# A graph layer on one core: one fixed order for the gather stage, readers further behind the gathers, and other buffers around it

## The chip, the cores and the metric

The kernel runs on one core of a Trainium2 chip. The metric is the device time of one execution in microseconds (us), smaller being better; the median of several runs is compared. A core has five engines with a program each: PE (TensorE, matrix products), DVE (VectorE), ACT (ScalarE), POOL (GpSimd) and SP (SyncE, here only an issuer of transfers). They run side by side and wait for one another by semaphores. Transfers (DMA) are issued from the queues of SP, ACT and POOL.

## The reference

A graph layer over 12500 nodes with 256 features and 200000 edges, sorted by their target node:

```python
h = relu(layernorm(x))                                   # 12500 x 256
agg = segment_sum(h[src], dst, num_segments=12500)       # 200000 gathered rows
z = (1 + eps) * h + agg
t = relu(batchnorm(z @ W1 + b1, g1, bt1))                # 12500 x 512
y = relu(batchnorm(t @ W2 + b2 + h, g2, bt2))            # 12500 x 256
return x + y
```

A batchnorm takes its mean and variance over all nodes, so each of the two ends a stage: nothing behind it can start before the last node's row is known.

## The kernel before

**Tiles.** The 200000 edges are 1563 tiles of 128, taken in 131 groups of GT = 12. As the edges are sorted by target, a group's targets lie close together: group i is taken to lie in a window of WIDE = 128 + 2 x 76 = 280 nodes that begins at 96 i - 76 (`span`, STEP = 96). A short stage at the start checks this on the device and sets a flag; a second program for other data (`general`) isn't run here. The 12500 nodes are 25 chunks of 512.

**Start.** dst and src are loaded as whole numbers (L146 to L158): each as a block of whole rows in one or two transfers, a short last row in one more, and the places behind it filled with zeros first. dst goes through SP's queue and DVE's fill, src through ACT's queue and POOL's fill; ACT's queue also carries the small vectors and the two weight matrices. They are turned so that each column holds one tile's indices; the checks and the flag follow.

**The gather stage** (most of the time). Its parts, by name:

- `gather(i)` (L391 to L401): twelve indirect transfers on POOL, L398, each fetching 128 rows by src into one buffer `gt`; there are AHEAD + 1 = 5 such buffers. For the first LEAD = 24 groups the rows come from x, and `settle` (L338 to L357) normalises them in place (six bn_stats on DVE, a root on ACT, reciprocal and product on DVE, twelve activations on ACT); later groups read the table h_tab.
- `h_chunk(g)` (L370 to L388): makes a chunk of h from x by the same `settle`, stores it in h_tab, transposes it on PE (L381), copies it out of PSUM (L385, L387) and stores it in h_cols.
- `sums(i)` (L419 to L436): DVE builds a 0/1 matrix `oh` from the targets (L423), PE adds up the group's rows per target in `ps` with twelve matmuls (L433), which the profile shows as 24 records.
- `join(i)`: ACT copies `ps` to `zs` (L440), DVE builds the placing matrix `at` (L442). `put(i)`: PE places the sums in the window, `pz` (L452). `add(i)`: DVE adds `pz` into the chunks `zc` that the window touches (L465). `z_chunk` loads such a chunk from h_cols and scales it by 1 + eps (L412).
- `first_layer(c)`: once no later window touches chunk c, PE multiplies it with W1 in four slices (L474), DVE takes bn_stats (L478), ACT copies the slice to `ts` (L479), and one transfer of 1 MB stores the chunk in t_tab (L480).

The loop L488 to L509 writes these down in the order h_chunk, gather(i+4), join(i-1), put(i-1), settle(i), sums(i), add(i-1), first_layer. The compiler's scheduler then sets each engine's order; on PE it places the first two tiles of the next group's sums ahead of put, and the rest behind it. Buffers: gt 5, oh 2, zs 3, at 2, ps 2, pz 1, ts 2.

**Second layer.** `ti` reads t_tab back and `yT` reads h_cols (SP's queue, L531, L532), ACT normalises (`tT`, L535), PE multiplies with W2 (L542), DVE adds h and takes statistics. Before its end, XAHEAD = 10 chunks of x are loaded. **Output.** ACT normalises (L560), PE transposes, DVE adds x, ACT's queue stores; each step loads one more chunk of x.

Of the kernel before, what the change touches and what calls it, by code (L numbers as in the profile page):

```python
# [7 lines left out]
F32 = mybir.dt.float32  # L8
I32 = mybir.dt.int32
AF = mybir.ActivationFunctionType  # L10
OP = mybir.AluOpType
PSUM = bass.MemoryType.PSUM
# [3 lines left out]
R = 4  # L16
EPS = 1e-5
GT = 12
MARGIN = 76
AHEAD = 4  # L20
LEAD = 24
XAHEAD = 10

# [7 lines left out]
def kernel(  # L31
# [103 lines left out]
    with ExitStack() as es:  # L135
# [7 lines left out]
        safe = whole // 32 * 32  # L143
        assert PU <= P and whole < PU and PU - safe <= 32
        raws = {}
        for name, arr, eng in (("d", dst, nc.sync), ("s", src, nc.scalar)):  # L146
            raws[name] = ti = raw.tile([P, PART], I32, name="rawi_" + name)
            (nc.vector if name == "d" else nc.gpsimd).memset(ti[safe:PU, :], 0)
            if safe:
                eng.dma_start(ti[:safe, :], arr[: safe * PART].rearrange("(p e) -> p e", e=PART))  # L150
            if whole > safe:
                eng.dma_start(
                    ti[safe:whole, :], arr[safe * PART : whole * PART].rearrange("(p e) -> p e", e=PART)
                )
            if rest:
                eng.dma_start(
                    ti[whole : whole + 1, :rest], arr[whole * PART :].rearrange("(o e) -> o e", o=1)
                )  # L158
# [121 lines left out]
    def fast():  # L280
# [24 lines left out]
        with ExitStack() as fs:  # L305
# [8 lines left out]
            with ExitStack() as es:  # L314
# [4 lines left out]
                tsp = es.enter_context(tc.tile_pool(name="ts", bufs=2))  # L319
                ps_h = es.enter_context(tc.tile_pool(name="ps_h", bufs=1, space=PSUM))  # L320
                ps_i = es.enter_context(tc.tile_pool(name="ps_i", bufs=1, space=PSUM))
                ps_s = es.enter_context(tc.tile_pool(name="ps_s", bufs=2, space=PSUM))
                ps_z = es.enter_context(tc.tile_pool(name="ps_z", bufs=1, space=PSUM))
                ps_t = es.enter_context(tc.tile_pool(name="ps_t2", bufs=2, space=PSUM))

                col_i = keep.tile([P, WIDE], I32, name="col_i")
# [32 lines left out]
                xts = {}  # L359
# [10 lines left out]
                def h_chunk(g):  # L370
                    n = chunks[g][1] * R
                    slots = len(parts[g])
                    x_chunk(g + 2)
                    ht = ln.tile([P, R, D], F32, name="ht")
                    settle(xts.pop(g), -(-slots // 2), slots, ht, "c")
                    carry(nc.scalar, ht, h_tab, g, store=True)
                    hc = ln.tile([P, DC, CH], F32, name="hc")
                    for d in range(DC):
                        ph = ps_h.tile([P, CH], F32, name="pc")
                        for c in range(slots):  # L380
                            nc.tensor.transpose(  # L381
                                ph[:, c * P : (c + 1) * P], ht[:, c, d * P : (d + 1) * P], ident
                            )
                        if d % 2:
                            nc.scalar.copy(hc[:, d, :n], ph[:, :n])  # L385
                        else:
                            nc.vector.tensor_copy(hc[:, d, :n], ph[:, :n])  # L387
                    nc.sync.dma_start(h_cols[g, :, :, :n], hc[:, :, :n])  # L388
# [15 lines left out]
                zc = {}  # L404

                def z_chunk(c):
                    if c in zc or c >= NCH:
                        return
                    n = chunks[c][1] * R
                    zc[c] = zcp.tile([P, DC, CH], F32, name="zc")  # L410
                    nc.sync.dma_start(zc[c][:, :, :n], h_cols[c, :, :, :n])
                    nc.scalar.activation(zc[c][:, :, :n], zc[c][:, :, :n], AF.Copy, scale=gin1)  # L412

                def span(i):
                    return STEP * i - MARGIN, STEP * i - MARGIN + WIDE

                summed, placed = {}, {}

                def sums(i):  # L419

                    t0, n = groups[i]
                    oh = sel.tile([P, GT, P], F32, name="oh")
                    nc.vector.tensor_tensor(  # L423
                        oh[:, :n, :],
                        col[:, :P].unsqueeze(1).to_broadcast([P, n, P]),
                        dstT[:, t0 : t0 + n].unsqueeze(2).to_broadcast([P, n, P]),
                        op=OP.is_equal,
                    )
                    ga = gathered.pop(i)
                    ps = ps_s.tile([P, D], F32, name="ps")  # L430
                    for j in range(n):
                        rows = left if t0 + j == full_tiles else P
                        nc.tensor.matmul(  # L433
                            ps, lhsT=oh[:rows, j, :], rhs=ga[:rows, j, :], start=(j == 0), stop=(j == n - 1)
                        )
                    summed[i] = ps  # L436

                def join(i):
                    zs = sel.tile([P, D], F32, name="zs", bufs=3)
                    nc.scalar.copy(zs, summed.pop(i))  # L440
                    at = sel.tile([P, WIDE], F32, name="at")
                    nc.vector.tensor_scalar(  # L442
                        at, col, shift[:, i : i + 1], None, op0=OP.is_equal
                    )
                    placed[i] = zs, at

                def put(i):

                    zs, at = placed.pop(i)
                    pz = ps_z.tile([P, DC, CH], F32, name="pz2")  # L450
                    for d in range(DC):
                        nc.tensor.matmul(  # L452
                            pz[:, d, :WIDE], lhsT=zs[:, d * P : (d + 1) * P], rhs=at, start=True, stop=True
                        )
                    return pz

                def add(i, pz):
                    lo, hi = span(i)
                    for c in range(max(lo, 0) // CH, -(-min(hi, N) // CH)):
                        z_chunk(c)  # L460
                        a, b = max(lo, c * CH, 0), min(hi, (c + 1) * CH, N)
                        if a >= b:
                            continue
                        side = zc[c][:, :, a - c * CH : b - c * CH]
                        nc.vector.tensor_add(side, pz[:, :, a - lo : b - lo], side)  # L465
                    z_chunk(max(lo, 0) // CH + 1)

                def first_layer(c):
                    n = chunks[c][1] * R
                    ts = tsp.tile([P, HC, CH], F32, name="ts")  # L470
                    for f in range(HC):
                        ph = ps_t.tile([P, CH], F32, name="ph")
                        for d in range(DC):
                            nc.tensor.matmul(  # L474
                                ph[:, :n], lhsT=w1s[:, d, f * P : (f + 1) * P],
                                rhs=zc[c][:, d, :n], start=(d == 0), stop=(d == DC - 1),
                            )
                        nc.vector.bn_stats(st1[:, f, c, :], ph[:, :n])  # L478
                        nc.scalar.copy(ts[:, f, :n], ph[:, :n])  # L479
                    nc.scalar.dma_start(t_tab[c, :, :, :n], ts[:, :, :n])  # L480
                    del zc[c]

                x_chunk(0)
                x_chunk(1)
                for i in range(min(AHEAD, NG)):
                    gather(i)
                made = done = 0
                for i in range(NG + 1):  # L488

                    while made < NCH and made < 2 + NCH * i // (LEAD - AHEAD):  # L490
                        h_chunk(made)
                        made += 1
                    if i + AHEAD < NG:
                        gather(i + AHEAD)
                    pz = None
                    if i > 0:
                        join(i - 1)
                        pz = put(i - 1)
                    if i < NG:
                        if i < LEAD:  # L500
                            settle(gathered[i], GT // 2, GT, gathered[i], "g")
                        sums(i)
                    if i == 0:
                        continue
                    add(i - 1, pz)
                    nxt = span(i)[0] if i < NG else N
                    while done < NCH and min((done + 1) * CH, N) <= nxt:
                        first_layer(done)
                        done += 1  # L509
# [4 lines left out]
            late = fs.enter_context(tc.tile_pool(name="late", bufs=1))  # L514
            yT = [late.tile([P, DC, w * R], F32, name=f"yT{g}") for g, (_, w) in enumerate(chunks)]

            xin = fs.enter_context(tc.tile_pool(name="xin", bufs=XAHEAD))
            xrs = []

            def x_rows(g):  # L520
                if g < NCH:
                    xrs.append(xin.tile([P, R, D], F32, name="xr"))
                    carry(nc.sync, xrs[g], x, g, store=False)

            with tc.tile_pool(name="tin", bufs=3) as tin, tc.tile_pool(name="tsb", bufs=2) as tsb, tc.tile_pool(
                name="ps_y", bufs=4, space=PSUM
            ) as ps_y:
# [26 lines left out]
            with tc.tile_pool(name="ysb", bufs=3) as ysb, tc.tile_pool(name="ps_o", bufs=3, space=PSUM) as ps_o:  # L554
                for g in range(NCH):
# [18 lines left out]
                    x_rows(g + XAHEAD)  # L574
# [251 lines left out]
```

## Time and profile before

| what | value |
|---|---|
| three runs | 2607.53, 2616.31, 2614.66 us |
| median | 2614.66 us |
| the profiled execution: time, and span in the trace | 2590.8 us, 2589.0 us |
| start, until the first gather | 26.35 us |
| gather stage: first gather to the end of the last | 26.35 to 2294.5 us |
| from there to the first matmul of the second layer | 2342.66 us |
| second layer, until the first output activation | 2515.29 us |
| output | to 2589.0 us |

A group of instructions is shown on the page as line, engine, operation, tiles written and read, number, busy time, mean ns of one, then the idle time of its engine just before them and what ended most of it. The row of slices gives a busy share in tenths for each fortieth of the span, 64.7 us. A row of the timeline gives start, length, engine, line and operation, and in brackets the idle time before it and what ended that. The granted TensorE clock over the whole run is 0.767 of full speed.

The waits that the trace adds up over the whole span (waiting engine and line, what ended the wait, us in total, times, longest):

```profile
ACT zs L440 <- remote: 1256.0, 76, 38.9
DVE oh L423 <- remote: 904.9, 75, 22.6
PEld pz L452 <- ACT zs L440: 686.3, 65, 38.2
```

"remote" is a releaser that the trace doesn't name. And two stretches, of the gather stage and of the second layer (start and end, length, then busy time and number of PE, PEld, DVE, ACT and POOL instructions, the granted clock, the DMA engines' share, GB/s):

```profile
1200.00:1400.00 200.00, 112.93 (x395) 84.08 (x393) 41.98 (x54) 11.46 (x22) 135.21 (x143) 0.77 0.36 110
2350.00:2400.00 50.00, 50.00 (x118) 22.20 (x117) 19.80 (x29) 20.83 (x29) 0.00 (x0) 1.00 0.88 330
```

### The profile page before, as it was taken

To read this page: it belongs to the slowest core of one execution; us is meant where nothing else is said; L and a number is where in the kernel's file an instruction comes from. 1 tells how busy PE (TensorE), PEld (TensorE's weight loads), DVE (VectorE), ACT (ScalarE), POOL (GpSimd) and SP (SyncE) were. 2 spreads that over 40 slices of the span, in tenths; PEclk is the share of its full clock that TensorE was granted. 3 is DMA by queue.
4 is the path that set the end of the run, shared out by engine and by line. 5 is a ranking of instruction groups with operands and counts; after the bars stand their busy time and mean duration, and the time that the engine had idled before them with its cause. 6 is when DMAs were issued, how large, how long until landed. Compare 5 with 4: busy or idle time off the path is not lost.

```text
span 2589.0 us, 14795 instructions
## 1 busy us (share of the span) xinstructions
PE 1435.9 (55%) x4873; PEld 1021.2 (39%) x4873; DVE 711.9 (27%) x1059; ACT 467.4 (18%) x885; POOL 1482.4 (57%) x1576
## 2 busy tenths in 40 slices
PE   1255575554654545464745544555564555478985
PEld 1243353432433334343534433443343434353444
DVE  5244464421221212121212211221121221133444
ACT  3254465500000000000000000000000000014434
POOL 4655466666666666666666666666666666720000
PEclk9667687776877777677877777777776777788996
DMA  6455575433333333333333333333333333328728
GB/s 193 141 179 166 175 232 161 132 113 95 118 120 113 93 121 115 91 118 119 114 95 120 113 119 94 115 114 92 121 116 92 117 112 110 96 78 335 265 85 301
DMA packets 147183, 349.41 MB, mean 135 GB/s; under 512 B 28917, under 2 KB 81241, under 8 KB 140953
## 3 DMA queue, kind: packets, MB, share of 16 engines
q0 software_dynamic: 75008, 204.90, 26.7%
q1 hardware_dynamic: 41146, 90.41, 10.2%
q10 hardware_dynamic: 30942, 53.06, 5.5%
q8 instruction: 41, 0.67, 0.1%
q14 instruction: 46, 0.37, 0.0%
HBM read 284.26 MB, written 64.00 MB: 135 GB/s over the span
## 4 chain that ended last, share of the span: by engine, by line
another core or an unknown queue 51%; PE 26%; ACT 7%; issue 7%; DMA 4%; DVE 3%; POOL 1%; ACTq 0%; SPq 0%; POOLq 0%; DVEq 0%
PE ps L433 10%; PE py L542 6%; PE ph L474 5%; PE pz L452 4%; ACT gt L355 3%; DMA out_dram<-ot 1%; ACT zs L440 1%; POOL gt L398 1%; DMA zc<-h_cols 1%; ACT ht L355 1%; ACT zc L412 1%; DVE oh L423 1%; DVE st L478 1%; PE po L566 1%
## 5 line engine op out<-in xcount | busy, mean ns | idle before, releaser
L398 POOL DMA_INDIRECT gt<-h_tab,srcT x1275 | 1206.2, 946 | 608.5 <-issue 371.9
L433 PE MATMUL ps<-gt,oh 128*128 128x256 f32 x3126 | 789.9, 414 | 74.9 <-ACT gt L355 61.1
L433 PEld LDWEIGHTS ps<-gt,oh 128*128 128x128 f32 x3126 | 665.2, 213 | 198.3 <-ACT gt L355 65.1
L452 PE MATMUL pz<-at,zs 128*128 128x280 f32 x524 | 215.9, 549 | 770.1 <-ACT zs L440 660.3
L423 DVE TENSOR_TENSOR oh<-col,dstT 128x1536 f32<-128x1536 f32 x131 | 229.0, 1748 | 1143.3 <-remote 904.9
L452 PEld LDWEIGHTS pz<-at,zs 128*128 128x128 f32 x524 | 123.2, 252 | 834.9 <-ACT zs L440 686.3
L398 POOL DMA_INDIRECT gt<-in_x_dram,srcT x288 | 273.0, 948 | 180.8 <-ACT zs L440 96.1
L440 ACT COPY zs<-ps 128x256 f32<-128x256 f32 x131 | 48.8, 372 | 1613.7 <-remote 1256.0
L474 PE MATMUL ph<-zc,w1s 128*128 128x512 f32 (+1 forms) x400 | 214.6, 689 | 188.7 <-issue 145.3
L474 PEld LDWEIGHTS ph<-zc,w1s 128*128 128x128 f32 x400 | 86.4, 225 | 298.4 <-issue 241.5
L465 DVE TENSOR_TENSOR zc<-pz,zc 128x560 f32<-128x560 f32 (+9 forms) x203 | 100.8, 526 | 340.6 <-remote 167.8
L542 PE MATMUL py<-tT,w2s 128*128 128x512 f32 (+1 forms) x400 | 169.6, 587 | 12.0 <-ACT tT L535 12.0
L355 ACT ACTIVATE gt<-gt,nbg,rsg 128x256 f32<-128x256 f32 x288 | 149.5, 590 | 4.1 <-DVE nbg L353 1.8
L542 PEld LDWEIGHTS py<-tT,w2s 128*128 128x128 f32 x400 | 76.4, 192 | 105.2 <-issue 86.9
L478 DVE BATCH_NORM_STATS2 st<-ph 128x6 f32<-128x512 f32 (+1 forms) x100 | 67.2, 681 | 154.3 <-PE ph L474 64.5
L344 DVE BATCH_NORM_STATS2 stg<-gt 128x6 f32<-128x512 f32 x144 | 91.5, 688 | 33.4 <-DMA gt<-in_x_dram,srcT 23.2
L479 ACT COPY ts<-ph 128x512 f32<-128x512 f32 (+1 forms) x100 | 57.4, 575 | 197.1 <-DVE st L478 147.3
L535 ACT ACTIVATE tT<-ti,of,sc 128x512 f32<-128x512 f32 (+1 forms) x100 | 72.1, 792 | 99.8 <-issue 90.7
L381 PE MATMUL pc<-ident,ht 128*128 128x128 f32 x196 | 39.3, 334 | 53.6 <-issue 22.0
L442 DVE TENSOR_SCALAR at<-col,shift 128x280 f32<-128x280 f32 x131 | 65.4, 499 | 0.3 <-PE pz L452 0.3
L546 DVE TENSOR_TENSOR yT<-py,yT 128x512 f32<-128x512 f32 (+1 forms) x50 | 33.9, 677 | 109.2 <-PE py L542 107.2
L381 PEld LDWEIGHTS pc<-ident,ht 128*128 128x128 f32 x196 | 28.5, 171 | 72.1 <-issue 28.5
(80 smaller groups left out, 396.9 us busy)
## 6 DMA issues: line engine op xcount, KB each, us to landing
t_tab<-ts ACTq DMA_DIRECT2D x24, 1024.0 KB
ti<-t_tab SPq DMA_DIRECT2D x24, 1024.0 KB
gt<-h_tab,srcT POOLq DMA_INDIRECT x1275
xt<-in_x_dram SPq DMA_DIRECT2D x24, 512.0 KB
h_tab<-ht ACTq DMA_DIRECT2D x24, 512.0 KB
h_cols<-hc SPq DMA_DIRECT2D x24, 512.0 KB
zc<-h_cols SPq DMA_DIRECT2D x24, 512.0 KB
yT<-h_cols SPq DMA_DIRECT2D x24, 512.0 KB
```

Of the source, the lines that this page charges most:

```text
L344: nc.vector.bn_stats(st[:, c : c + 2, :].rearrange("p c s -> p (c s)"), v[:, c : c + 2, :].rearrange("p c d -> p d c"),)
L355: nc.scalar.activation(to[:, c, :], v[:, c, :], AF.Relu, bias=nb[:, c : c + 1], scale=rs[:, c : c + 1])
L398: nc.gpsimd.indirect_dma_start(out=ga[:rows, t - t0, :], out_offset=None, in_=x if i < LEAD else h_tab, in_offset=bass.IndirectOffsetOnAxi ...
L423: nc.vector.tensor_tensor(oh[:, :n, :], col[:, :P].unsqueeze(1).to_broadcast([P, n, P]), dstT[:, t0 : t0 + n].unsqueeze(2).to_broadcast([P ...
L433: nc.tensor.matmul(ps, lhsT=oh[:rows, j, :], rhs=ga[:rows, j, :], start=(j == 0), stop=(j == n - 1))
L440: nc.scalar.copy(zs, summed.pop(i))
L452: nc.tensor.matmul(pz[:, d, :WIDE], lhsT=zs[:, d * P : (d + 1) * P], rhs=at, start=True, stop=True)
L465: nc.vector.tensor_add(side, pz[:, :, a - lo : b - lo], side)
L474: nc.tensor.matmul(ph[:, :n], lhsT=w1s[:, d, f * P : (f + 1) * P], rhs=zc[c][:, d, :n], start=(d == 0), stop=(d == DC - 1),)
L478: nc.vector.bn_stats(st1[:, f, c, :], ph[:, :n])
L535: nc.scalar.activation(tT[:, f, :n], ti[:, f, :n], AF.Relu, bias=of1[:, f : f + 1], scale=sc1[:, f : f + 1],)
L542: nc.tensor.matmul(py[:, :n], lhsT=w2s[:, f, d * P : (d + 1) * P], rhs=tT[:, f, :n], start=(f == 0), stop=(f == HC - 1),)
```

## The change

- **Window.** MARGIN is 64 for 76, so WIDE is 256 for 280, which the data still fits.
- **Edge loads.** dst and src both go through SP's queue, each as one block, one short row, and one more transfer that fills the rest of that row with edges from the front of the array; no zero fill.
- **Order.** In the gather stage the scheduler no longer orders: each engine runs the instructions as they are written. A step i is: gather(i+4); add(i-4); `take` (bn_stats, copy and store) of the slice made in the step before; spots(i-2) and hold(i-2), the two halves of the old join; edges(i+1), which builds `oh`; h_chunk(i); settle(i+1); z_scale; sums(i); the transposes and copies of chunk i-1 (`turn`, `turn_out`); put(i-2); z_load; and at most one slice of the first layer.
- **Buffers.** oh 3, at 3, ht 3, ps 3, pz 2. `ts` holds one slice, four of them, each stored by its own transfer of 256 KB. The transposes share the slices' two PSUM buffers.
- **Lead-in.** LEAD is 30 for 24; one chunk of h per step for 25 steps instead of 25 in 20 steps.
- **Later stages.** The buffers of ti, tT and four more x chunks lie at the other end of the memory, apart from the gather stage's, and each tile waits for its own place to come free rather than for a whole pool. Four more chunks of x (XMORE) are loaded before the output stage.

```diff
-MARGIN = 76
+MARGIN = 64
-LEAD = 24
+LEAD = 30
+XMORE = 4
...
+        for name, arr in (("d", dst), ("s", src)):
+            raws[name] = ti = raw.tile([P, PART], I32, name="rawi_" + name)
+            nc.sync.dma_start(ti[:whole, :], arr[: whole * PART].rearrange("(p e) -> p e", e=PART))
+            for at, e0, n in ((0, whole * PART, rest), (rest, 0, PART - rest)):
+                if n:
+                    nc.sync.dma_start(
+                        ti[whole : whole + 1, at : at + n], arr[e0 : e0 + n].rearrange("(o e) -> o e", o=1)
+                    )
...
-                ps_h = es.enter_context(tc.tile_pool(name="ps_h", bufs=1, space=PSUM))
-                ps_s = es.enter_context(tc.tile_pool(name="ps_s", bufs=2, space=PSUM))
-                ps_z = es.enter_context(tc.tile_pool(name="ps_z", bufs=1, space=PSUM))
+                ps_s = es.enter_context(tc.tile_pool(name="ps_s", bufs=3, space=PSUM))
+                ps_z = es.enter_context(tc.tile_pool(name="ps_z", bufs=2, space=PSUM))
+                es.enter_context(tc.manual_schedule())
...
+                def take(c, f):
+                    n = chunks[c][1] * R
+                    ph = slices.pop((c, f))
+                    nc.vector.bn_stats(st1[:, f, c, :], ph[:, :n])
+                    ts = tsp.tile([P, CH], F32, name="ts")
+                    nc.scalar.copy(ts[:, :n], ph[:, :n])
+                    nc.scalar.dma_start(t_tab[c, :, f, :n], ts[:, :n])
...
+                for i in range(NG + 4):
+                    before = added
+                    if i + AHEAD < NG:
+                        gather(i + AHEAD)
+                    late = 4 if i < NG else 3
+                    while added <= min(i - late, NG - 1):
+                        add(added)
+                        added += 1
+                    for c, f in taken:
+                        take(c, f)
+                    taken = []
+                    if 0 <= i - 2 < NG:
+                        spots(i - 2)
+                        hold(i - 2)
+                    if i + 1 < NG:
+                        edges(i + 1)
+                    if i < NCH:
+                        h_chunk(i)
+                    if i + 1 < min(LEAD, NG):
+                        settle(gathered[i + 1], GT // 2, GT, gathered[i + 1], "g")
+                    for c in scales.get(i, ()):
+                        z_scale(c)
+                    if i < NG:
+                        sums(i)
+                    if 0 < i <= NCH:
+                        turn(i - 1)
+                        turn_out(i - 1)
+                    if 0 <= i - 2 < NG:
+                        put(i - 2)
+                    for c in loads.get(i, ()):
+                        z_load(c)
...
-            with tc.tile_pool(name="tin", bufs=3) as tin, tc.tile_pool(name="tsb", bufs=2) as tsb, tc.tile_pool(
+            with tc.tile_pool(name="tin", bufs=3, side="right", reuse_waits="tile") as tin, tc.tile_pool(
+                name="tsb", bufs=2, side="right", reuse_waits="tile"
...
+                for g in range(XAHEAD, XAHEAD + XMORE):
+                    x_rows(g)
...
-                    x_rows(g + XAHEAD)
+                    x_rows(g + XAHEAD + XMORE)
```

## The prediction

> **What bounds the kernel now.** I read the page's shares first, then the slices, the groups, the waits, and last the timeline of one stretch.
>
> ```profile
> span 2589.0 us, 14795 instructions
> PE 1435.9 (55%) x4873; PEld 1021.2 (39%) x4873; DVE 711.9 (27%) x1059; ACT 467.4 (18%) x885; POOL 1482.4 (57%) x1576
> POOL 4655466666666666666666666666666666720000
> DMA  6455575433333333333333333333333333328728
> ```
>
> No engine is full. GpSimd is at six tenths in every slice until it ends in slice 36, so nearly the whole span is one stage that POOL's gathers run through; the DMA engines are a third busy there, so bytes don't set it. The groups and waits say what POOL lacks:
>
> ```profile
> L398 POOL DMA_INDIRECT gt<-h_tab,srcT x1275 | 1206.2, 946 | 608.5 <-issue 371.9
> L398 POOL DMA_INDIRECT gt<-in_x_dram,srcT x288 | 273.0, 948 | 180.8 <-ACT zs L440 96.1
> L452 PE MATMUL pz<-at,zs 128*128 128x280 f32 x524 | 215.9, 549 | 770.1 <-ACT zs L440 660.3
> ...
> POOL gt L398 <- issue: 453.9, 1478, 2.1
> POOL gt L398 <- remote: 206.3, 53, 6.2
> POOL gt L398 <- ACT zs L440: 105.7, 17, 15.0
> ```
>
> A gather takes 0.95 us and an issue gap of 0.30; between waits the timeline has their starts 1.25 us apart, and twelve, one group, take 15.0 us. 1563 gathers at 1.2508 are 1955 us. The first starts at 26.35 and the last ends at 2294.5, which is 2268: POOL waits 313 us. In two windows: up to 480 us, 288 gathers in 454 us against 360 (94 lost); from 480 to 2294.5, 1275 in 1814.5 against 1595 (220 lost). So a group takes 17.1 us in the long part, not 15.0. The one bound that stays if every wait goes is 15.0.
>
> What POOL waits for is a free gt buffer, which the sums of five groups earlier release. The landed data is four groups ahead, so the chain sums, zs copy, at, pz, add is late:
>
> ```profile
> 1207.89 5.34 PE L433 MATMUL ps<-gt,oh 128*128 128x256 f32 x24
> ...
> 1227.61 0.95 POOL L398 DMA_INDIRECT gt<-h_tab,srcT  x1 [0.30 <-issue]
> 1231.87 0.37 ACT L440 COPY zs<-ps 128x256 f32<-128x256 f32 x1 [25.21 <-remote]
> 1231.87 1.76 DVE L423 TENSOR_TENSOR oh<-col,dstT 128x1536 f32<-128x1536 f32 x1 [21.96 <-remote]
> 1232.11 0.94 POOL L398 DMA_INDIRECT gt<-h_tab,srcT  x1 [3.55 <-remote]
> 1232.30 2.23 PE L452 MATMUL pz<-at,zs 128*128 128x280 f32 x4 [19.06 <-ACT zs L440]
> ```
>
> The matmuls are recorded as over at 1213.2, yet zs (ACT), the next oh (DVE) and POOL all go on only at 1231.9, with PE idle between. Other groups go on at once. I found no cause in the trace; the lateness of PE's completion is the unknown that decides this case. In the order of before it holds up everything, as pz of a group stands in front of the next group's sums and waits for its zs.
>
> **Part 1, the order of the stage.** A step now makes sums(i), then put(i-2), then at most one slice of the first layer; adds come four behind, gathers four ahead; oh, zs, at, ps, pz have two or three buffers. What is left of the wait is judged by each engine's load. PE: in the window 480 to 2280 it is busy 940.9 us for 106 groups, 8.9 a group, sums, pz and slices together. DVE 365.4 (3.4 a group) and ACT 121.5 (1.1). All stand under 15.0, so in the steady part POOL should be the bound; gather(i+4) needs sums(i-1), which leaves PE nearly three groups, 45 us, for a lateness of up to 24. Worth: the 220 us. 1275 x 1.2508 = 1595.
>
> A rule that speaks against this: PEclk reads 0.75 in that window. The Trainium skill ("TensorE: Matmul & The Clock Gate", Part 1) says that an idle window of about 3.4 us drops the clock to half and about 3.4 us of work brings it back. The new order spreads PE's work over each step with some 6 us free, so the gate could close in every step. By the row, a group costs 8.9. By the rule at its worst, half clock throughout, 8.9 x 0.75 / 0.5 = 13.4 us, an estimate, still below 15.0. I take the row: the clock moves PE but not the end.
>
> **Part 2, lead-in of 30 groups and one chunk of h per step.** Six more settled groups add 6 x (6 x 0.688) = 25 us to DVE and 6 x (12 x 0.59) = 42 to ACT; both lie beside POOL's 15.0 a group. The question is one step's ping-pong with both a chunk and a group. ACT: ts 0.58, zs 0.37, root 0.29, a DVE answer 0.34, four ht 2.36, a wait for six bn_stats (4.10 less 2.36), root 0.30, answer 0.36, twelve gt 7.09, zc scale 1.14, hc 0.58: 15.15, with hops 15.6. From the other side, with sums at half clock (24 x 0.43 = 10.3, the slow records of that group, whose mean is 0.414) the DVE copy of hc, which now waits behind them, delays the next step: 12.3 + 0.7 + 5.1 of DVE's work ahead of the next root, less 1.24, is 16.9. Over 25 steps: (15.6 - 15.0) x 25 = 15 to (16.9 - 15.0) x 25 = 47 us, of which gathers run ahead hide some 27. Loss 0 to 37; I take 10, where before loses 94. h_tab's last chunk is made in step 24 (about 25 x 15.6 + 40 = 430); gather(30) comes at 23.5 + 360 x 1.2508 = 474, so the table is there.
>
> **Part 3, slices, ts and t_tab.** 100 stores of 256 KB for 25 of 1 MB. The rule against it ("SBUF — State Buffer", The DMA setup-cost knee): each transfer pays about 2 us however small, so coalesce. By the rule: 75 more x 2 = 150 us if it were serial. By the rows: an issue on ACT's queue takes 0.33, 75 more are 25 us on an engine with 1.1 us of work per 15 us step, and a 1 MB load (ti) starts tT 5.0 us after issue, so a quarter of it lands well within a step with four ts buffers. Cost 0; without that cover, in the last eight slices, 0 to 5 us.
>
> **Part 4, the end of the stage.** From the last gather's end to the first second-layer matmul before: 2342.66 - 2294.5 = 48.2, of which five waiting groups take some 30 (6.1 us each) and the ti load ends last:
>
> ```profile
> 2336.75 11.14 SPq L531 DMA_DIRECT2D ti<-t_tab  x5
> 2341.79 5.75 ACT L535 ACTIVATE tT<-ti,of,sc 128x512 f32<-128x512 f32 x8 [9.09 <-DMA ti<-t_tab]
> ```
>
> ti, tT now lie apart from the stage's buffers, so the loads can come before the norm is done (2333.5): 8 us go. No backlog: landing 2, last sums 1.7, three hops of hold, put, add at 2.5, a chunk's four slices 7.0, the last chunk with norm 6.7, tT 0.9: 26. I take 30 (23 to 42).
>
> **Part 5, the start.** src's small loads are issued at 10.37 and 10.82, behind ten other loads on ACT's queue, its cast starts at 16.01, the flag falls at 24.27, of which DVE's rel (until 18.1) bounds part. On SP's queue behind dst they come by about 9, so the cast by 13. Two fills (1.48 POOL, 1.45 DVE) go, two small loads come. Gain 2.5 to 3, bounds -4 to +5; I take the first gather at 23.5.
>
> **Part 6, more x early.** Second layer: PE back to back, unchanged. In the last 74 us DMA's share is 0.81, so 2 MB of x that move ahead of it are worth 0 (hidden) to 2 MB / 277 GB/s = 7.6; I take 3. WIDE 256 for 280: pz and at shrink by 9%, off the path.
>
> **Sum.** 23.5 + 1955 + 10 = 1988.5; + 30 = 2018.5 for the second layer; before's rest, 2589.0 - 2342.66 = 246.3, less 3: 2262 of span. The profiled run was 2590.8, 1.8 over its span: 2264. The runs' median, 2614.66, is 0.9% above the profiled run; whether that lies in waits that go or in the pace I can't tell, so I add two thirds: **2280**.
>
> **Rivals.**
> - *PE's lateness is PE's own, and still ends part of the steps.* For: it strikes three waiters at once, and nothing in the order explains it. Against: from 2291, gathers over, five groups ran at 6.1 us without it. hold(i-2) waits behind the ts copy of the last slice, so a slice late by 19 makes a step of 19 + 5 = 24, one on time 10; if 45% are late, 16.3 on the mean. Over 101 groups: 2280 + 1.3 x 101 = **2410**. If all of the 17.1 stays, only lead-in, tail and start gain: 2280 + 2.1 x 101 = 2490.
> - *Slower: the fixed order chains the engines.* In each step ACT's hold, DVE's edges and the bn_stats stand behind the same slice, and next the sums behind edges; a late slice stops all three, where the scheduler's order had something between. Four of five steps late: 0.8 x 24 + 0.2 x 10 = 21.2, over 101 groups 2280 + 6.2 x 101 = **2906**. It decides against the change from a mean step of 15.0 + (2615 - 2280) / 101 = 18.3, that is, when about 60% of slices are late. Before, 63 of 106 zs in the long window waited on "remote", 18 us each, which is near that point; but most of those stand behind pz, and two groups' slack wasn't there.
> - *It does nothing:* the waits only change their names, the order being data-bound. Lead-in, tail and start alone would still give 2490, so within 0.3% (which is about what a measurement can tell from none) needs a loss that cancels them: **2610**.
>
> **Chances.** Forecast 0.55 (own range 2240 to 2340), PE's lateness 0.28 (2340 to 2490), slower 0.14, nothing 0.03. The range runs over the first two, to 2470. Faster 0.84, same 0.02, slower 0.14.
>
> **What would show it.** Right: POOL near eight tenths in its slices, gather idle by issue alone (0.30 a gather), the last gather by 2000, zs idle without effect on POOL, ti landed before the norm's end. Part 2 wrong: POOL waits before 480 us on gt. Rival one: POOL still waits on "remote" or PE after 500 us, 16 us a group. Slower: the waits name ts or oh, and POOL falls under six tenths.

## The result, and the profile after

The medians of five runs each are 2564.79 us after and 2610.16 before. The ratio is 0.9824, with a 95% interval of 0.9803 to 0.9844. The change gains 1.8%, 45 us, a seventh of the 335 us forecast. The profiled run spans 2563.9 us, against 2589.0 before. Three lines of its page and three of its waits (waiting engine and line, what ended the wait, us in total, times, longest):

```profile
POOL 4666666666666666666666666666666666610000
...
L406 POOL DMA_INDIRECT gt<-h_tab,srcT x1203 | 1138.6, 947 | 565.3 <-issue 364.0
...
L467 PE MATMUL pz<-at,zs 128*128 128x256 f32 x524 | 176.8, 461 | 430.2 <-ACT zs L456 330.5
```

```profile
DVE st L496 <- remote: 914.4, 45, 37.8
POOL gt L406 <- issue: 481.3, 1503, 5.7
POOL gt L406 <- remote: 195.8, 36, 6.6
```

POOL is still at six tenths and still loses 196 us to a releaser without a name. The wait has a new name on DVE: bn_stats of the slice, first in the new order to need PE, waits where zs did.

The same trace shows what such a wait is made of. From the timeline (start, length, engine, operation, idle time before it), with lines left out:

```profile
1199.73 2.54 PE L449 MATMUL ps<-gt,oh 128*128 128x256 f32 x11
...
1203.27 0.47 PE L449 MATMUL ps<-gt,oh 128*128 128x256 f32 x1 [0.34 <-issue]
...
1206.06 0.38 PE L449 MATMUL ps<-gt,oh 128*128 128x256 f32 x1 [1.73 <-issue]
...
1212.25 0.94 POOL L406 DMA_INDIRECT gt<-h_tab,srcT  x1 [0.30 <-issue]
1213.06 0.58 PE L449 MATMUL ps<-gt,oh 128*128 128x256 f32 x1 [2.21 <-issue]
1215.15 0.58 PE L449 MATMUL ps<-gt,oh 128*128 128x256 f32 x1 [1.51 <-issue]
1216.55 2.14 PE L449 MATMUL ps<-gt,oh 128*128 128x256 f32 x4 [0.81 <-issue]
1217.40 0.70 DVE L496 BATCH_NORM_STATS2 st<-ph 128x6 f32<-128x512 f32 x1 [24.54 <-remote]
1217.52 0.94 POOL L406 DMA_INDIRECT gt<-h_tab,srcT  x1 [4.33 <-remote]
```

The first eleven matmul records follow one another at 0.22 us. Then they come singly, and their starts lie whole multiples of 0.70 us apart (1203.27 to 1213.06 is 14 x 0.70), up to 2.80 us from one to the next. POOL's last gather ends at 1213.2; 3.4 us later PE's records are close together again (elsewhere in this trace steps come up to 6 us after POOL's last gather). I call this the **hold-up**: PE waits for no semaphore that the trace shows, yet advances in steps. The granted clock doesn't explain it: from 1202 to 1207 us it was 1.0, and PE was busy 2.1 of these 5 us. The hold-up can also be invisible, as the ends of matmul records are modelled: in the stretch shown of the kernel before, all 24 records looked normal and only the completion was 19 us late.

### The profile page after: what moved, and what is told of

It is laid out like the page before. It is cut to its first block, busy times and chain, and to the rows that moved or that the text cites. A ratio compares the mean times of both kernels' runs of the same rounds, so it can differ in the third digit from the quotient of the medians.

```text
span 2563.9 us, 14957 instructions
## 1 busy us (share of the span) xinstructions
PE 1505.5 (59%) x4873; PEld 1021.2 (40%) x4873; DVE 713.6 (28%) x1090; ACT 506.3 (20%) x963; POOL 1482.7 (58%) x1575
## 4 chain that ended last, share of the span: by engine, by line
POOL 38%; issue 19%; another core or an unknown queue 16%; PE 12%; DVE 7%; ACT 5%; DMA 2%; ACTq 0%; DVEq 0%; POOLq 0%; SPq 0%
POOL gt L406 38%; PE py L606 7%; ACT gt L353 3%; DVE stg L342 2%; PE ps L449 2%; PE ph L485 2%; DVE oh L435 1%; DMA out_dram<-ot 1%; PE po L634 1%; PE pz L467 1%; DVE stc L342 1%; DVE st L496 1%; ACT ht L353 1%; DVE ot L640 0%
## 5 line engine op out<-in xcount | busy, mean ns | idle before, releaser
L406 POOL DMA_INDIRECT gt<-h_tab,srcT x1203 | 1138.6, 947 | 565.3 <-issue 364.0
L449 PE MATMUL ps<-gt,oh 128*128 128x256 f32 x3126 | 894.9, 432 | 461.2 <-issue 353.5
L406 POOL DMA_INDIRECT gt<-in_x_dram,srcT x360 | 342.5, 951 | 182.5 <-issue 117.3
L467 PE MATMUL pz<-at,zs 128*128 128x256 f32 x524 | 176.8, 461 | 430.2 <-ACT zs L456 330.5
L485 PE MATMUL ph<-zc,w1s 128*128 128x512 f32 (+1 forms) x400 | 237.6, 726 | 68.4 <-DVE hc L395 42.9
L353 ACT ACTIVATE gt<-gt,nbg,rsg 128x256 f32<-128x256 f32 x360 | 180.2, 586 | 16.2 <-issue 9.4
L478 DVE TENSOR_TENSOR zc<-pz,zc 128x512 f32<-128x512 f32 (+8 forms) x187 | 93.6, 519 | 248.3 <-remote 160.6
L342 DVE BATCH_NORM_STATS2 stg<-gt 128x6 f32<-128x512 f32 x180 | 111.9, 686 | 17.7 <-DMA gt<-in_x_dram,srcT 14.6
L460 DVE TENSOR_SCALAR at<-col,shift 128x256 f32<-128x256 f32 x131 | 61.5, 470 | 0.0
L634 PE MATMUL po<-ident,yr 128*128 128x128 f32 x196 | 38.2, 376 | 30.8 <-ACT yr L628 30.8
```

Of the source, the lines that this page charges most:

```text
L342: nc.vector.bn_stats(st[:, c : c + 2, :].rearrange("p c s -> p (c s)"), v[:, c : c + 2, :].rearrange("p c d -> p d c"),)
L353: nc.scalar.activation(to[:, c, :], v[:, c, :], AF.Relu, bias=nb[:, c : c + 1], scale=rs[:, c : c + 1])
L406: nc.gpsimd.indirect_dma_start(out=ga[:rows, t - t0, :], out_offset=None, in_=x if i < LEAD else h_tab, in_offset=bass.IndirectOffsetOnAxi ...
L449: nc.tensor.matmul(ps, lhsT=oh[:rows, j, :], rhs=ga[:rows, j, :], start=(j == 0), stop=(j == n - 1))
L467: nc.tensor.matmul(pz[:, d, :], lhsT=zs[:, d * P : (d + 1) * P], rhs=at, start=True, stop=True)
L485: nc.tensor.matmul(ph[:, :n], lhsT=w1s[:, d, f * P : (f + 1) * P], rhs=zc[c][:, d, :n], start=(d == 0), stop=(d == DC - 1),)
```

## The experiments

Each run is a single execution, beside one of the kernel before on the same chip. That second number decided how to read the first: on four chips the kernel before took 2263 to 2265 us, on three others 2604 to 2620. I call them *free* and *held* chips. No chip was used twice, so whether a chip is always held, or was so at that time, is not shown, nor what else ran on it. The last column says whether the trace shows PE free or held up.

| run | what | us | kernel before beside it | PE in the trace |
|---|---|---|---|---|
| e1_half_tiles | half of the sums' matmuls | 2266 | 2264 | free |
| e2_one_gather | one gather per group from 30 on | 1505 | 2264 | free |
| e3_zero_oh | one-hot all zero | 2273 | 2264 | free |
| e4_half_cols | half of the columns in the sums | 2264 | 2264 | free |
| c1_before | kernel before | 2620 | 2607 | held |
| c2_after | changed kernel | 2561 | 2607 | held |
| c3_zero_oh | one-hot all zero | 2552 | 2607 | held |
| d1_half_tiles, d2_one_gather, d3_fill | repeats, and more matmuls | 2269, 1504, 2272 | 2265 | free |
| d4_after | changed kernel | 2271 | 2265 | free |
| f1_before | kernel before, traced | 2263 | 2263 | free |
| f2_half_tiles, f3_fill | repeats | 2276, 2278 | 2263 | free |
| g1_phases | four stretches in one run | 2425 | 2620 | held |
| k1_phases2 | four other stretches | 1981 | 2604 | held |
| h1_ahead6 | seven gt buffers | 2576 | 2604 | held |
| m1_paced | gathers spaced out | 2450 | 2264 | free |

**First chip: four edits to the changed kernel.** The sums' loop, for e1 (e2 also cuts the gathers to one, e3 adds 0.5 to dstT, e4 takes `ga[:rows, j, :P]`):

```diff
-                    for j in range(n):
+                    for j in range(0, n, 2):
```

> The changed kernel, with only every second tile of a group multiplied in the sums (six of twelve; the other gathered rows are fetched and left out of the result). All waits, buffers and gathers stay. Theory PE (what PE gets done beside the gathers is limited, 17.0 us a group in both orders): less PE work per group, so POOL's own pace of 15.0 us a group rules and the time falls to about 2290 us (2260 to 2330). Theory order (some wait of the order or a buffer sets 17.0): the waits are all still there, 2500 us or more.

> The changed kernel, from group 30 on with one gather per group instead of twelve; the sums multiply all twelve one-hot blocks with that one gathered tile, so PE's work is the same and the other rows are left out of the result. Theory PE alone (PE is limited whatever runs beside it): groups still take 17.0 us, about 2540 us in all. Theory traffic (it is the gathers beside it that hold PE up): groups fall to about 9 to 10 us, PE's recorded work, about 1800 us in all.

> The changed kernel with 0.5 added to the relative targets, so that no entry of the one-hot matrices is 1: the sums multiply by zeros and the aggregate is left out of the result; every instruction, wait and transfer stays. Theory power (PE is held back by what its arithmetic draws): no hold-up, about 2290 us. Every theory in which the data doesn't matter: 2565 us, within 10.

> The changed kernel with the sums over 128 of the 256 feature columns (the other half is left out; the placing uses the first half twice): as many PE instructions and weight loads as before, half the columns streamed. If PE is limited by columns streamed: about 2290 us. If by instructions or weight loads: about 2560 us. Theory order: 2500 us or more.

Taken alone, e1, e3 and e4 each match a theory, and all three at once: 2266, 2273, 2264. But the kernel before took 2264 beside them. The chip had no hold-up to take away, and none of the three says anything of it. Of e2 one figure stands: with one gather a group PE was busy all of 640 us (560 to 1200), at 7.3 us a group, where 9 to 10 were expected.

**Second chip: both kernels as they are, and the zeros.**

> The kernel before, unchanged. In the runs just made its time beside them was 2264 us, not 2610. Theory chip (PE is held up on some chips or at some times and not on others, and that hold-up, not the order, is what the first profile showed): either 2264 with no late completion of PE in the trace and POOL waiting only at the issue gap after 500 us, or about 2610 with PE's completions late by up to 20 us. Theory order (the order alone makes the wait): about 2610.

> The changed kernel, unchanged. Theory chip: where the kernel before takes 2264, this one is at POOL's pace too, 2260 to 2290; where that takes 2610, this one takes 2565. Theory order: 2565 wherever it runs.

> The changed kernel with zeros for the one-hot matrices, as before. If this call's kernel before takes about 2610: theory power 2270, theory chip without power 2565. If it takes about 2264, this run says nothing of PE's hold-up and takes 2270.

A held chip: 2620, 2561, and with zeros 2552. The kernel before, unchanged, takes 2264 us on one chip and 2620 on another, so "order" falls and "chip" holds, the chip or its state. "Power" falls as far as it is the sums' one-hot operand that would draw it: 9 us of 290.

**Third and fourth chip: both free.** f3 and d3 add to the changed kernel:

```diff
+                        if i >= LEAD:
+                            for _ in range(5):
+                                nc.tensor.matmul(extra, lhsT=ident, rhs=w1s[:, 0, :], start=True, stop=True)
```

> The changed kernel with five more matmuls of 128x512 in each step from group 30 on, whose result is left out, so that PE has some 13 us of work per step instead of 9 and idles less (ps has two buffers for three, to make room in PSUM). Where the kernel before takes about 2610: theory budget 17.0 x 13.2 / 8.9 = 25 us a group, 3300 us; theory start: fewer bursts after idle, 2300 to 2450. Where it takes about 2264: 2265 to 2330, as PE stays under POOL's 15.0.

> The changed kernel, unchanged, once more beside the kernel before. Where that takes about 2264: this one is at POOL's pace as well, 2255 to 2285. Where that takes 2610: 2565.

> The kernel before, unchanged, for its trace. Theory chip: where it takes about 2265, POOL waits at the issue gap alone, groups at 15.0 us in the long part, and no zs copy starts more than 1 us after the last recorded matmul of its group; where it takes about 2610, the late completions again.

2272, 2271, 2263. The traces of d4 and f1 show both orders without the hold-up. Changed kernel (d4), its page and waits:

```profile
span 2269.4 us, 14957 instructions
...
POOL 4777777777777777777777777777777777600000
...
L467 PE MATMUL pz<-at,zs 128*128 128x256 f32 x524 | 136.8, 384 | 5.0 <-ACT zs L456 5.0
```

```profile
POOL gt L406 <- issue: 469.8, 1542, 0.4
...
POOL gt L406 <- DMA gt<-in_x_dram,srcT: 1.8, 6, 0.3
```

and the kernel before on a free chip (f1), the same two views:

```profile
span 2261.4 us, 14795 instructions
...
POOL 4777777777777777777777777777777777700000
...
L452 PE MATMUL pz<-at,zs 128*128 128x280 f32 x524 | 223.1, 568 | 11.6 <-ACT zs L440 11.3
```

```profile
POOL gt L398 <- issue: 468.6, 1538, 0.4
```

In both POOL waits for hardly anything but its issue gap; the 770 us for which PE stood idle ahead of pz in the old order are 12. One group of f1, to set beside the one that the prediction shows:

```profile
1199.88 5.34 PE L433 MATMUL ps<-gt,oh 128*128 128x256 f32 x24
...
1205.26 0.37 ACT L440 COPY zs<-ps 128x256 f32<-128x256 f32 x1 [1.17 <-PE ps L433]
1205.26 1.76 DVE L423 TENSOR_TENSOR oh<-col,dstT 128x1536 f32<-128x1536 f32 x1 [4.02 <-PE ps L433]
```

The 24 records are as long as on the held chip, but zs and the next oh start when they end. From group 24 on no zs of f1 starts more than 0.1 us after the last recorded matmul of its group; in the first profile 59 of 106 start over 3 us after it. On a free chip the scheduler's order, one group behind the gathers, never held POOL up, and there was nothing in it to win. What the change costs on a free chip is at the end of the stage. Kernel before (f1), then changed (d4):

```profile
1987.19 7.03 PE L474 MATMUL ph<-zc,w1s 128*128 128x512 f32 x16
...
2013.96 3.63 ACT L535 ACTIVATE tT<-ti,of,sc 128x512 f32<-128x512 f32 x5 [9.27 <-DMA ti<-t_tab]
```

```profile
1999.72 7.03 PE L485 MATMUL ph<-zc,w1s 128*128 128x512 f32 x16
...
2022.64 2.93 ACT L599 ACTIVATE tT<-ti,of,sc 128x512 f32<-128x512 f32 x4 [3.93 <-DMA t_tab<-ts]
```

The last full chunk's slices start 12.5 us later, though the last gather ends 1 us earlier (1979.0 against 1980.1): the readers that stand two to four groups behind have to be caught up. From the norm's last instruction to tT the kernel before needs 8.5 us and the changed one 3.1, since ti is there early; the last store of t_tab is then what ends the wait. Together the stretch from the last gather to the second layer grows from 34.7 to 44.5 us.

**Fifth chip: four stretches in one execution,** so that a held chip tells all at once. From g1 (ps also has two buffers):

```diff
+                    step = 2 if 55 <= i < 80 else 1
-                    for j in range(n):
+                    for j in range(0, n, step):
...
+                        if 80 <= i < 105:
+                            for _ in range(5):
+                                nc.tensor.matmul(extra, lhsT=ident, rhs=w1s[:, 0, :], start=True, stop=True)
```

> The changed kernel with four stretches in one run: groups 30 to 54 as they are; 55 to 79 with every second tile of the sums left out; 80 to 104 with five more matmuls of 128x512 per step, their result left out; from 105 on one gather per group, the sums multiplying that tile twelve times (ps has two buffers for three). Read by the start of the first gather of groups. Where the kernel before takes about 2610: theory budget 17.0, 15.0, 25, 17 us a group; theory start 17.0, over 16.5, 15 to 16, 10. Where it takes about 2265: 15.0, 15.0, 15.0, 10, about 2130 us in all.

A held chip. The windows, one inside each stretch (start and end, length, busy us and number for PE, PEld, DVE, ACT, POOL, the granted clock, DMA share, GB/s):

```profile
600.00:1000.00 400.00, 220.64 (x736) 161.55 (x735) 79.84 (x109) 36.00 (x71) 266.26 (x281) 0.77 0.37 109
1010.00:1410.00 400.00, 150.25 (x478) 108.00 (x476) 74.03 (x95) 22.24 (x44) 266.59 (x282) 0.69 0.38 111
1440.00:1830.00 390.00, 287.64 (x852) 178.08 (x853) 74.31 (x97) 22.33 (x44) 258.95 (x274) 0.82 0.38 109
1870.00:2100.00 230.00, 197.03 (x764) 147.29 (x764) 77.00 (x100) 24.40 (x48) 21.78 (x23) 0.98 0.13 43
```

Read POOL's count: 281, 282 and 274 gathers are 1.423, 1.418 and 1.423 us a gather, 17.0 to 17.1 us a group (the first gathers of groups 30, 55, 80 and 105 say the same: 17.0, 17.1, 17.1), although PE has 221, 150 and 288 us of work. PE runs some three groups behind, so the first 50 us of a window still hold PE's work of the stretch before. Half the sums gain nothing and five more matmuls a step cost nothing. "Budget" falls (15.0 and 25 expected). "Start" gave 17.0 and over 16.5 rightly, but fill should have fallen to 15 or 16. In the last stretch, one gather per group, the hold-up is gone: 0.98 of the full clock and 9.8 us a group, with two ps buffers (e2, with three, took 7.3).

**Sixth chip: what in the gathers does it.** From k1:

```diff
+                    some = 1 if 30 <= i < 80 else 6 if 80 <= i < 105 else n
-                    for t in reversed(range(t0, t0 + n)):
+                    for t in reversed(range(t0, t0 + some)):
...
+                    if 30 <= i < 55:
+                        for _ in range(11):
+                            nc.gpsimd.memset(waste, 0.0)
+                    if 55 <= i < 80:
+                        for j in range(1, n):
+                            nc.sync.dma_start(ga[:, j, :], h_tab[(8 * i + j) * P % 12000 : (8 * i + j) * P % 12000 + P, :])
```

> The changed kernel with four other stretches: groups 30 to 54 with one gather per group and eleven fills of 128x1050 on POOL, about 1 us each, in place of the other gathers; 55 to 79 with one gather and eleven plain loads of 128 rows on SP's queue; 80 to 104 with six gathers; from 105 on twelve as usual. The sums multiply twelve one-hot blocks everywhere, with the tiles that are there, so other rows are left out of the result. PE is called held up where zs starts over 3 us after the last recorded matmul of its group, or its matmuls come in steps of 0.70 us. Where the kernel before takes about 2610: theory gathers (only POOL's indirect transfers in an unbroken row do it) first two stretches free, 10 to 13 us a group, six gathers free or nearly, the last 17.0; theory POOL busy: the first held up as well; theory traffic: the second held up as well. Where it takes about 2265: about 12.5, 10, 10, 15.0.

A held chip; the same kind of windows:

```profile
620.00:880.00 260.00, 199.59 (x732) 153.28 (x731) 74.63 (x96) 22.89 (x45) 240.13 (x247) 0.89 0.16 51
890.00:1070.00 180.00, 174.74 (x733) 139.68 (x733) 76.98 (x99) 22.58 (x45) 40.33 (x43) 0.99 0.78 239
1090.00:1320.00 230.00, 188.46 (x729) 143.49 (x727) 72.39 (x96) 22.54 (x44) 152.20 (x161) 0.91 0.43 122
1400.00:1660.00 260.00, 147.13 (x473) 100.43 (x471) 44.95 (x58) 13.64 (x26) 175.31 (x186) 0.72 0.38 108
```

The first sign named above can't be used. In the new order zs stands behind other work, and starts over 3 us after its group's last matmul on a free chip too (d4: 99 of 106 groups). The bn_stats of a slice is a better sign: in d4 all 68 between 560 and 1900 us start 0.04 us after the slice's last recorded matmul; in the profiled run of the result 38 of 60 start over 1 us after it. In the four windows of k1 these are 0 of 18, 0 of 17, 8 of 17 and 5 of 10, and 2, 0, 16 and 56 matmul starts lie at a multiple of 0.70 us (within 0.02) from the one ahead.

With POOL busier than in any gather stretch (240 of 260 us) and PE at work beside it, then, no hold-up: 11.3 us a group. With more than twice the DMA traffic, from SP's queue (239 GB/s against 108), none either: PE is busy 175 of 180 us, 7.6 us a group. With twelve gathers, 300 take 426 us from 1251 on, 1.42 us each. Six gathers are not free. The third window runs past their stretch, as POOL begins with twelve at 1251; so here is one from the first gather of group 80 to that of group 105:

```profile
1035.50:1251.10 215.60, 195.07 (x786) 151.84 (x785) 83.71 (x109) 25.48 (x50) 141.79 (x150) 0.96 0.46 130
```

150 gathers in 215.6 us are 8.6 us a group and 1.44 us a gather, where POOL needs 7.5 us a group and PE took 7.6 in the stretch before; from 1090 to 1250 us, 6 of 14 slices are late. So neither POOL's being busy with fills nor traffic as such does it; the indirect transfers do, at six a group as well, where POOL still issued up to 18 without a pause. "Gathers" holds in this, but not in "six gathers free". Whether the row has to be unbroken, and what in these transfers it is (their scattered rows, their queue, their number), is not separated.

**More buffers.** `AHEAD = 6`, `LEAD = 32`, on the same held chip:

> The changed kernel with gathers six groups ahead and seven gt buffers instead of four and five (LEAD 32 for the chunks of h). Where the kernel before takes about 2610: theory company (PE is held up while gathers run on and let go some 4 us after POOL stops for want of a buffer, so each pause of 6 us is paid once per set of buffers) 75 + 6 us per five groups, 16.2 a group, about 2480; theory share (PE simply gets less done) 17.0 a group as before, 2565. Where it takes about 2265: 2265 to 2280.

2576, no gain, so "company" falls in its price: two more groups in hand don't spread the pauses. With five buffers (the run of the result) as with seven, POOL mostly issues 36 gathers, three groups, and then pauses for 6.1 to 6.4 us: 21 of 31 and 20 of 32 pauses between 560 and 1900 us are of this length. Counted between 560 and 1900 us, POOL's gathers are:

| kernel | chip | gathers in 1340 us | us each |
|---|---|---|---|
| before | held | 947 | 1.415 |
| after | held | 945 | 1.418 |
| c1_before | held | 932 | 1.438 |
| c2_after | held | 948 | 1.414 |
| c3_zero_oh | held | 949 | 1.412 |
| h1_ahead6 | held | 945 | 1.418 |
| f1_before | free | 1073 | 1.249 |
| d4_after | free | 1073 | 1.249 |

On held chips the changed kernel's four runs, with two depths of buffers, stand within 0.5% of one another, and the old order 0 to 2% behind them; on free chips the two orders are equal.

**Seventh chip: spaced gathers.** A small fill on POOL behind each gather, four paces:

> The changed kernel with the gathers spaced out by a small fill on POOL after each: groups 30 to 54 about 1.42 us a gather, 55 to 79 about 1.32, 80 to 104 about 1.55, from 105 on 1.25 as it is. The result is whole. Where the kernel before takes about 2610: theory rate (PE is held up only while gathers follow one another faster than some pace near 17.0 / 12 = 1.42) no steps of 0.70 us and no pauses of POOL in the first and third stretch, 17.0 and 18.6 us a group, and in the second 15.8 if 1.32 is slow enough; theory any gathers: steps of 0.70 us in all four and more than 12 gathers' time a group. Where it takes about 2265: 17.0, 15.8, 18.6, 15.0 and PE free throughout, about 2425 us.

A free chip, 2450 us, with 17.2, 16.1, 18.7 and 15.0 us a group and PE free throughout, so whether a slower row keeps PE free on a held chip is not shown. It stays open, and with it what in the chip makes the hold-up. That there is a limit of 1.41 to 1.44 us a gather in the long run, and PE's lateness only shows it, fits all held runs; but how the one brings about the other is not shown. The transfers themselves are not later: a gather's first packet starts 1.65 us and its last 2.4 us after POOL's instruction begins (medians), in the two profiles of the result as in f1 and d4.

## Why the prediction was wrong, point by point

Measured against its sum, in us of the span. "Held" is the profiled run of the result, "free" is d4:

| term | forecast | held | free |
|---|---|---|---|
| first gather | 23.5 | 25.9 | 24.1 |
| 360 gathers of the lead-in | 460.3 | 527.7 | 451.7 |
| 1203 gathers from h_tab | 1504.7 | 1700.9 | 1503.2 |
| to the second layer | 30 | 64.2 | 44.5 |
| the rest | 243.3 | 245.3 | 245.9 |
| span | 2262 | 2563.9 | 2269.4 |

- **The step that failed is Part 1**: "What is left of the wait is judged by each engine's load ... so in the steady part POOL should be the bound; gather(i+4) needs sums(i-1), which leaves PE nearly three groups, 45 us, for a lateness of up to 24. Worth: the 220 us." It took PE's late completion for a delay that a deeper pipeline hides. The runs show a rate instead: on a held chip 17.0 to 17.4 us a group whatever the order, the work of PE or the buffers. What sets that rate stays open. The 220 us were never the order's, as f1 shows by not having them. The miss there is 196 us, in the lead-in 67, at the end 34: 297 of 302.
- The first rival named the right thing, that the lateness stays, but priced it at 2410 by letting buffers and luck keep half of it away; even its upper end, 2490, kept the gains of lead-in and tail, of which the held chip gave 31 us of 84 and none. My argument against it was "from 2291, gathers over, five groups ran at 6.1 us without it". That line was the clue: it says what the lateness needs. I read it as a sign that it would go.
- **Lead-in**: on a free chip hardly a pause (451.7 us against 450.3 for 360 gathers without any), against 10 us taken; the ping-pong that I priced at 15.6 us a group kept up with 15.0. But f1 starts its 361st gather at 476.8 too, so the 94 us "lost" by the old lead-in were the hold-up's as well. On the held chip the new one does gain: group 30's first gather starts at 553.5 against 584.8, 31 us earlier, more than the whole difference of the two profiled spans (25). In c1 and c2, on one chip, 40 of 59 us come before group 30 and 30 from there to the last gather, and the end takes 12 back.
- **The end of the stage**: the step "no backlog: landing 2, last sums 1.7, three hops of hold, put, add at 2.5" is the mis-sized term, 30 against 44.5. The last full chunk's slices began 20.7 us after the last gather, not some 11. The early ti was right in kind and gave 5.4 us of 8. And the 48.2 of before held the backlog of the hold-up: without it the old order needs 34.7. So the change loses 10 us here on a free chip and 16 between the profiled runs of the result.
- **Start**: 2.0 us gained on a free chip, 0.5 in the profiled pair, 2.85 forecast. **More x early**: the output takes 2.1 us less on a free chip and 1.8 in the profiled pair, 3 forecast. Both right in kind; but the second layer, put at unchanged, takes 1.5 and 0.8 more.
- **The clock rule** (the Trainium skill, "TensorE: Matmul & The Clock Gate", Part 1): the estimate from it was 13.4 us a group at the worst, below 15.0. On the free chip (d4) the clock is 0.81 from 500 to 1900 us, PE is busy 9.6 us a group, and it waits for gathers. **The rule on small stores** ("SBUF — State Buffer", The DMA setup-cost knee): no sign of the 150 us, which were an estimate from that section's 2 us a transfer; 75 more stores cost nothing but at the end, where a store of ts is the last to let tT go.
- Slower and nothing: the first didn't happen. The second is what a free chip gives, 2271 against 2265, for a reason that I hadn't named: no waits to remove.

## What to carry to other kernels

A consumer that stays late whatever its own work may be waiting for a rate, not for a distance; more buffers hide a delay and not a rate. Before pricing a reordering, look in the same trace for stretches in which the lateness is absent and ask what else is absent there: here the gathers were. And run the unchanged kernel beside every experiment, on the same chip: without its 2264 us, three edits on the first chip would each have passed as the cure.

## What the runs showed of the hardware

- On three of the experiments' seven chips, and in both profiles of the result, PE falls behind while indirect transfers follow one another at 1.25 us. In the changed kernel's records single matmuls then start 0.70 us or a multiple of it apart, mostly up to 2.80: 241 in the profiled run between 560 and 1900 us, of them 211 of sums, 21 of placing and 9 of slices, the last some 6 us after a row of gathers ended. Eleven POOL fills or eleven plain loads per group in the gathers' place don't bring it about (no late slice in 18 and 17).
- On those chips the gathers' own long-run pace was 1.41 to 1.44 us, over two orders, two depths of buffers, half and more of PE's work, and six or twelve gathers a group; on the others it was 1.25 us.
- The records of the matmuls alone can hide this: in the stretches shown of the kernel before, 24 of them take 5.34 us on a held and on a free chip. The next instruction of another engine that needs PE shows it, 19 us later on the one and at once on the other.
